# Attention block with FFN on one core: v ahead of q and k, the next norm in steps behind v's tiles, weight sums only in the attention

## The chip, the cores and the metric

The kernel runs on one core of a Trainium2 chip. The metric is the device time in microseconds of one execution; the time given is the median of several executions. The engines are named as in the profile: PE is TensorE (PEld its weight loads), DVE VectorE, ACT ScalarE, POOL GpSimd, SP SyncE. SP computes nothing here and issues DMAs on a hardware queue (q1 in the profile); DMAs issued from POOL go through a software queue (q0).

## The reference

x has the shape (2, 2048, 1024), that is 4096 tokens of H = 1024 in two batches. Everything is fp32.

```python
x = x + attn(layernorm(x), Wqkv, bqkv, Wo, bo)
x = x + ffn(layernorm(x), ...)

def attn(x, Wqkv, bqkv, Wo, bo):          # one head, D = 256
    qkv = x @ Wqkv + bqkv                 # (B, S, 3, 256)
    q, k, v = qkv[:, :, 0], qkv[:, :, 1], qkv[:, :, 2]
    p = softmax((q @ k.T) / sqrt(256))
    return (p @ v) @ Wo + bo

def ffn(h, ...):
    logits = h @ gate_w                   # 8 experts, the top 2 logits are summed
    w = sum(top_k(logits, 2))
    shared = (relu(h @ up_w) ** 2) @ down_w          # 1024 -> 2048 -> 1024
    routed = (((h @ fc1_w) @ expert_w) * w) @ fc2_w  # latent 512
    return layernorm(shared + routed) * ln_gamma + ln_beta
```

## The kernel before

**Matmuls in three passes.** TensorE gets every fp32 operand as a high part, rounded to its fp32r format, and a low part, the rest. `Pass3` (L117 to L138) adds high x high, high x low and low x high into one PSUM bank, so every product costs three matmuls; they are issued at L130. `split` (L140) makes the two parts: a cast on ACT (L142) and a subtraction on DVE or POOL (L143). `split_late` (L149, L150) does the same a step later, at the next `flush`.

**Blocks.** The 4096 tokens are 8 blocks of 512 (`NBLK` = 8, four per batch, `BPB` = 4), each of NB = 4 tiles of 128 rows. The stages are: the q/k/v stage for all blocks, the attention for all blocks, the FFN. The q/k/v stage takes the second batch first (`order`), since the k and v of the first batch can stay in SBUF (`keep`) for the attention that comes first; those of the second are written to `k_d` and `v_d` in DRAM and read back.

**The norm of a block.** x must be normalised by row, and TensorE needs it transposed, with features on the partitions. `norm_block` does this with four tiles of rows: the statistics of a tile come from ACT (`Moments`: two passes with a sum as they go, L259 and L271) or from DVE (`Stats`: bn_stats, L178 and L180) in turn; ACT normalises a tile in place (L283); DVE transposes it in 32x32 squares (`transpose_write`, L213), and POOL writes it to a DRAM scratch `xt_d` (L218); `fetch_tile` (L224) reads the tile back so that the squares come into their places. `split_tile` (L230) then splits a fetched tile into the high and low x (xha, xla) of the block that comes next.

**q, k and v of a block.** `qkv_block` does q as two chunks of 128 features by 512 tokens (24 matmuls 128x512 each, 8 contraction chunks in three passes; PSUM name pq), then k in the same way, then v as four tiles of 128 tokens by 256 features (24 matmuls 128x256 each, name pv). They share a PSUM pool, `psa`, of four banks. ACT evicts q and k (bias added), DVE the low half of k and all of v. q goes to `q_d` from POOL's queue. A callback `after` is called behind k and behind each v tile. `a_block` fills it: behind k come the loads of the rows of block i+2 (on SP's queue) and the split of tiles 0 and 1 of the next block, behind v tile 0 that of tile 2, behind v tile 1 that of tile 3. The norm of the block after that is called when the whole block is through:

```python
for i in range(NBLK - 1):
    if i:
        xts = norm_block(rows)
    xT = a_block(i, xts, xT)
```

This loop runs under `tc.manual_schedule()`: on each engine the instructions stay in the order in which they are written. Block 7's `a_block`, the attention and all behind it are ordered by the framework's scheduler from the program's order and priorities. In block 7 the callback behind k issues the scores of attention block 0 and its softmax's first quarter, ahead of the v tiles.

**Before the loop.** `begin` multiplies expert_w into fc2_w (`fold`), loads and splits the three parts of Wqkv (w0, w1 and w2 for q, k and v; subtractions on POOL, DVE and POOL), and makes the first block's x. The folded weights are written to `fc2e` from POOL's queue behind block 0.

**Weight sums.** The FFN uses sums of quarters of its weights, which are made in DRAM by DMAs alone, from POOL's queue: `sum_step` copies (2.5 MB per step) and adds (again 2.5 MB, an accumulating DMA). There are 14 steps, 8 of them with an add. Three steps are issued in the loop behind blocks i = 4, 5 and 6; the rest in the attention, two for each n from 2 on, behind the last `bo` DMA of the output projection before:

```python
if k in (2, 8) and n > 1 and steps:
    with tc.issue_after(last[0].ins):
        sum_step(steps.pop(0))
```

**The attention.** Its loop runs n from 1 to 8: scores of block n (name ps) beside values of block n-1 (name po), 16 key tiles of 128 each, with the softmax in quarters; `row_max` uses two small transposing matmuls (pmx, pmb) and `finish` the sums (psum, L604). `project` (L615 on) multiplies by Wo (name pw), adds the residual row `xres` (loaded on SP, with `bo` added by a POOL DMA) and writes x1 on SP (L634). In the last pass, n = 8, the four tiles of the FFN's first block are fetched on SP (name xt) and split on ACT and DVE (xh L149, xl L150), between the softmax quarters of the last attention block.

Of the kernel before, what the change touches and what calls it, by code (L numbers as in the profile page):

```python
# [12 lines left out]
ALU = mybir.AluOpType  # L13
# [4 lines left out]
P = 128  # L18
# [7 lines left out]
def kernel(  # L26
# [60 lines left out]
    def row(name):  # L87
        return rp.tile([P, C], FP, tag="r", name=name)
# [4 lines left out]
    def bank(pool, name):  # L93
        return pool.tile([P, W], FP, tag="b", name=name)
# [116 lines left out]
    def transpose_write(r, q=nc.gpsimd):  # L211
        b = row("xblk")
        nc.vector.transpose(  # L213
            b.rearrange("p (q k i) -> p q k i", q=P // SQ, i=SQ),
            r.rearrange("p (k i q) -> p q k i", k=NCC, i=SQ),
        )
        d = dram.tile([P, C], FP, tag="xt", name="xt_d", bufs=8)
        q.dma_start(out=d, in_=b)  # L218
        return d

    def fetch_tile(d, q=nc.gpsimd):

        xt = row("xt")
        q.dma_start(  # L224
            out=xt.rearrange("p (a f) -> p a f", a=P // SQ),
            in_=d.rearrange("(a i) (q f) -> (i q) a f", i=SQ, q=P // SQ),
        )
        return xt
# [65 lines left out]
        def second(self):  # L294
            pass

    def norm_block(rows):

        xts, ds = [], []
        ms = [Stats(r) if t % 2 else Moments(r, "n") for t, r in enumerate(rows[:2])]  # L300
        ms[0].second()
        for t in range(NB):
            ms[t].normalise()
            if t == 0:
                ms.append(Moments(rows[2], "n"))
                ms[2].second()
            ds.append(transpose_write(rows[t]))
            if t:
                xts.append(fetch_tile(ds[t - 1]))
            else:  # L310
                ms.append(Stats(rows[3]))
        return xts + [fetch_tile(ds[-1])]

    def transpose_tile(r, t, xT):

# [81 lines left out]
    def hl(t):  # L397

        return t.rearrange("p (s n) -> p s n", s=2)

    def qkv_block(n, wqkv, xT, after):

        keep = n < BPB
        units = {a: (unit if n == BPB - 1 else ex_unit)(f"{a}{n}") for a in "kv"}
        q = row("q")
        for i, a in enumerate("qk"):
            for dc in range(NDC):
                f = i * NDC + dc
                pm = bank(psa, "pq")
                acc = Pass3(pm, NCC)  # L410
                for c in range(NCC):
                    acc.add(piece(wqkv[i], c, D, ts(dc, P)), x_chunk(xT, c))
                bias = bqk_sb[:, f : f + 1]
                if a == "q":
                    nc.scalar.activation(q[:, ts(dc, W)], pm, AF.Identity, bias=bias)
                else:
                    h, l = (hl(units[a])[:, s, ts(dc, W)] for s in range(2))
                    nc.scalar.activation(h, pm, AF.Identity, bias=bias)
                    nc.vector.scalar_tensor_tensor(l, pm, bias, f32(h), ALU.add, ALU.subtract)
            if a == "q":  # L420
                nc.gpsimd.dma_start(out=q_d[n], in_=q)
            elif not keep:
                nc.gpsimd.dma_start(out=k_d[n], in_=f32(units[a]))
        if keep:
            kv[n] = [units["k"], units["v"]]
        after(-1)
        for t in range(NB):
            pm = bank(psa, "pv")
            if t % 2 == 0:
                v = half("v")  # L430
            acc = Pass3(pm[:, :D], NCC)
            for c in range(NCC):
                acc.add(x_chunk(xT, c, ts(t, P)), piece(wqkv[2], c, D, slice(0, D)))
            vt = v[:, ts(t % 2, D)]
            nc.vector.tensor_tensor(vt, pm[:, :D], bv_sb, ALU.add)
            flush()
            split_late(vt, *(hl(units["v"])[:, s, ts(t, D)] for s in range(2)))
            after(t)
        flush()
        if not keep:  # L440
            nc.gpsimd.dma_start(out=v_d[n], in_=f32(units["v"]))

    order = list(range(BPB, NBLK)) + list(range(BPB))
    def begin(wqkv, xT):

        ew, f2_0 = (unit(a, FP) for a in ("ew", "f2_0"))
        ev = ew.rearrange("p (c n) -> p c n", n=LAT)
        for i in range(NLC):
            nc.sync.dma_start(out=ev[:, :, ts(i, P)], in_=cols(expert_w, i, P))
        for i in range(NLC):  # L450
            nc.sync.dma_start(out=f2_0[:, ts(i, W)], in_=fc2_w[ts(i, P), 0:W])
        f2 = [f2_0]
        first = load_block(xf, order[0])
        f2.append(load("f2_1", cols(fc2_w, 1, W))[1])
        ws = [load(f"w{i}", cols(Wqkv, i, D)) for i in range(2)]
        rows = load_block(xf, order[1])
        ws.append(load("w2", cols(Wqkv, 2, D)))
        nc.gpsimd.dma_start(out=bqk_sb, in_=bqkv[0 : 2 * D].rearrange("(f p) -> p f", p=P))
        nc.gpsimd.dma_start(out=bv_sb, in_=bqkv[2 * D : 3 * D].partition_broadcast(P))

        eh, el = unit("eh"), unit("el")
        for mc in range(NLC):
            pt = bank(psc, "pt")
            for lc in range(NLC):
                nc.tensor.transpose(pt[:, ts(lc, P)], ew[:, ds(lc * LAT + mc * P, P)], ident)
            split(pt, eh[:, ts(mc, LAT)], el[:, ts(mc, LAT)])

        def split_f2(h, eng):
            f2h, f2l = unit(f"f2h{h}"), unit(f"f2l{h}")
            for mc in range(NLC):  # L470
                split(f2[h][:, ts(mc, W)], f2h[:, ts(mc, W)], f2l[:, ts(mc, W)], eng)
            return f2h, f2l

        def fold(f2hl, first=None):
            accs = [Pass3(bank(psa, "pf"), NLC) for _ in range(NLC)]
            for mc in range(NLC):
                if first:
                    first(mc)
                for lc in range(NLC):
                    accs[lc].add(  # L480
                        piece((eh, el), mc, LAT, ts(lc, P)), piece(f2hl, mc, W, slice(0, W))
                    )
            return accs

        def folded(h, accs):
            r = unit(f"fold{h}", FP)
            for lc in range(NLC):
                nc.scalar.copy(r[:, ts(lc, W)], accs[lc].ps)
            return r

        accs = fold(split_f2(0, nc.vector))
        stats = [row_stats(first[0])]
        for t in range(NB):
            if t + 1 < NB:
                stats.append(row_stats(first[t + 1]))
            normalise(first[t], stats[t])
            if t == 0:
                f2hl = split_f2(1, nc.gpsimd)
            elif t == 2:
                wqkv.append(split_unit(*ws[0], nc.gpsimd))  # L500
        r = [folded(0, accs)]
        r.append(folded(1, fold(f2hl, lambda t: transpose_tile(first[t], t, xT))))
        wqkv.append(split_unit(*ws[1]))
        wqkv.append(split_unit(*ws[2], nc.gpsimd))
        return norm_block(rows), r


    def split_q(n, r):
# [124 lines left out]
                )  # L633
            nc.sync.dma_start(out=x1[n][ts(t, P), :], in_=r)  # L634

    def a_block(i, xts, xT):
        nxt = []

        def after(t):

            if i + 1 < NBLK:
                if t < 0:
                    nxt.append(new_xT(f"a{i}"))
                    if i + 2 < NBLK:
                        rows[:] = load_block(xf, order[i + 2])
                for a in {-1: (0, 1), 0: (2,), 1: (3,)}.get(t, ()):
                    split_tile(xts[a], a, nxt[0])
            elif t < 0:
                start(0, load_row(q_d[0]))
                for k in range(NKC):  # L650
                    scores(0, k)
                start(1, load_row(q_d[1]))
                row_max(0)
                softmax(0, 0)

        qkv_block(order[i], wqkv, xT, after)
        return nxt[0] if nxt else None

    wqkv, xT = [], new_xT("a")
    with tc.manual_schedule():  # L660
        xts, fold = begin(wqkv, xT)
        steps = list(range(len(COPIES)))
        rows = []
        for i in range(NBLK - 1):
            if i:
                xts = norm_block(rows)
            xT = a_block(i, xts, xT)
            if i == 0:
                for h in range(C // W):
                    nc.gpsimd.dma_start(  # L670
                        out=cols(fc2e, h, W), in_=fold[h].rearrange("p (c n) -> p c n", n=W)
                    )
            if i >= NBLK // 2:
                sum_step(steps.pop(0))
    a_block(NBLK - 1, None, xT)

    wo_f = [load_row(Wo[ts(dc, P), :]) for dc in range(NDC)]

# [550 lines left out]
```

## Time and profile before

| | us |
|---|---|
| median of 3 runs | 2451.09 (2450.27 to 2451.32) |
| the profiled execution | 2448.58 |
| its span | 2446.8 |
| PE busy | 2360.8 (96%) |
| DVE busy | 1500.3 (61%) |
| ACT busy | 1133.7 (46%) |
| POOL busy | 338.5 (14%) |
| mean granted TensorE clock | 0.987 |

The span is that of one execution as the hardware profiler saw it; the 1.8 us between it and the execution's own time lie around it. Busy time counts computing instructions and not the waits. In the profile a line number is that of the kernel as it ran; "a <- b" in a wait reads "a waited for b". A program name such as xt or pq is that of a tile. In lists of stretches the columns are the stretch, its length, the busy time of the engines, the granted clock as a share of full clock, the busy share of the 16 DMA engines and the rate in GB/s.

### The profile page before, as it was taken

What the parts mean: (1) busy time and instruction counts of PE and PEld (TensorE: products, weight loads), DVE (VectorE), ACT (ScalarE), POOL (GpSimd) and SP (SyncE); (2) the same over time, 40 slices, a digit from 0 to 9 for tenths busy, and PEclk for the clock granted to TensorE, in tenths of its full rate; (3) what the DMA queues carried; (4) which work ended last, traced back from release to release, by engine and by line L of the source; (5) the groups of instructions that cost most, each with busy time, mean ns of one, the idle gap of its engine ahead of it and who ended that gap; (6) DMA issues with size and microseconds to landing.
All of it is one profiled execution on the core that took longest, in us unless ns stands there. A gap on an engine that the chain in (4) does not pass through costs nothing.

```text
span 2446.8 us, 29266 instructions
## 1 busy us (share of the span) xinstructions
PE 2360.8 (96%) x10704; PEld 1928.1 (79%) x10704; DVE 1500.3 (61%) x2168; ACT 1133.7 (46%) x1846; POOL 338.5 (14%) x427
## 2 busy tenths in 40 slices
PE   8899999999998999999999999999999999999997
PEld 7787888888886778777777877777888877787885
DVE  5555548888886466677845457663446673434646
ACT  5455435555544553666553364544135454214234
POOL 3211210111110010111320001221000021000003
PEclk9999999999999999999999999999999999999998
DMA  5866747999996566677887778986557787555565
GB/s 196 290 236 235 268 120 190 261 327 320 294 283 184 201 227 189 207 253 240 287 276 234 241 253 311 325 293 227 192 186 269 256 313 247 188 195 181 192 220 201
DMA packets 221342, 587.73 MB, mean 240 GB/s; under 512 B 18272, under 2 KB 80224, under 8 KB 219152
## 3 DMA queue, kind: packets, MB, share of 16 engines
q1 hardware_dynamic: 155616, 346.60, 42.3%
q0 software_dynamic: 65584, 239.27, 30.8%
q8 instruction: 85, 1.39, 0.2%
q14 instruction: 57, 0.47, 0.1%
HBM read 432.70 MB, written 210.76 MB: 263 GB/s over the span
## 4 chain that ended last, share of the span: by engine, by line
PE 72%; DVE 8%; DMA 7%; ACT 6%; issue 5%; POOL 1%; SPq 0%; POOLq 0%; ACTq 0%; DVEq 0%
PE pu L130 27%; PE pd L130 21%; PE ps L130 7%; PE po L130 7%; PE pw L130 4%; DMA xt<-xt_d 3%; DVE xblk L213 2%; DMA w<-wt 2%; DVE sp L996 1%; ACT xrow L283 1%; PE pg L829 1%; DMA xt_d<-xblk 1%; PE pf L130 1%; PE pq L130 1%; ACT junk L271 1%
## 5 line engine op out<-in xcount | busy, mean ns | idle before, releaser
L130 PE MATMUL pd<-w,sp 128*128 128x512 f32 x3336 | 775.3, 393 | 23.0 <-DVE sp L996 15.5
L130 PEld LDWEIGHTS pd<-w,sp 128*128 128x128 f32 x3336 | 626.1, 189 | 171.7 <-DVE sp L996 29.0
L130 PE MATMUL pu<-xh,w 128*128 128x512 f32 x2240 | 693.0, 390 | 2.0 <-ACT h L1026 1.0
L130 PEld LDWEIGHTS pu<-xh,w 128*128 128x128 f32 x2240 | 419.1, 188 | 93.2 <-DVE w L780 2.3
L130 PE MATMUL pu<-xl,w 128*128 128x512 f32 x1120 | 436.5, 390 | 3.7 <-DVE xl L150 3.7
L996 DVE TENSOR_TENSOR sp<-h,sp 128x512 fp32r<-128x512 f32 x238 | 178.0, 755 | 118.1 <-ACT sp L991 117.9
L130 PEld LDWEIGHTS pu<-xl,w 128*128 128x128 f32 x1120 | 210.2, 188 | 49.1 <-DVE xl L150 5.4
L991 ACT CAST sp<-h 128x512 fp32r<-128x512 f32 x238 | 144.9, 618 | 178.8 <-PE pd L130 127.3
L772 ACT CAST w<-w 128x512 fp32r<-128x512 f32 x210 | 128.7, 617 | 176.3 <-DMA w<-wt 163.2
L780 DVE TENSOR_TENSOR w<-w 128x512 fp32r<-128x512 f32 x210 | 147.0, 705 | 90.7 <-ACT w L772 85.8
L130 PE MATMUL po<-p,v 128*128 128x512 f32 x768 | 197.0, 395 | 1.3 <-ACT p L142 1.2
L130 PE MATMUL ps<-q,k 128*128 128x512 f32 x768 | 195.1, 392 | 0.0
L130 PEld LDWEIGHTS po<-p,v 128*128 128x128 f32 x768 | 144.3, 190 | 31.8 <-ACT p L142 1.6
L130 PEld LDWEIGHTS ps<-q,k 128*128 128x128 f32 x768 | 142.5, 188 | 32.1 <-DVE max L547 1.9
L783 POOL DMA_DIRECT2D w_p<-w x140 | 75.1, 536 | 562.9 <-DVE w L780 471.6
L150 DVE TENSOR_TENSOR xl<-xt,xh 128x512 fp32r<-128x512 f32 x104 | 77.5, 746 | 120.9 <-ACT xh L149 120.7
L213 DVE STREAM_TRANSPOSE xblk<-xrow 128x1024 f32<-128x1024 f32 x60 | 120.5, 2008 | 39.0 <-ACT xrow L283 39.0
L944 ACT ACTIVATE h<-h 128x1024 f32<-128x1024 f32 x48 | 50.7, 1055 | 200.6 <-DVE h L1043 153.2
L542 ACT COPY s<-ps 128x512 f32<-128x512 f32 x128 | 75.1, 587 | 147.1 <-PE ps L130 146.8
L908 POOL TENSOR_TENSOR res<-res,gb 128x1024 f32<-128x1024 f32 x32 | 80.1, 2506 | 408.0 <-DMA res<-x 407.6
L130 PE MATMUL pq<-xha,w_h 128*128 128x512 f32 x256 | 104.5, 408 | 20.9 <-ACT xha L142 20.9
L547 DVE TENSOR_TENSOR max<-ps,max 128x512 f32<-128x512 f32 x120 | 82.5, 688 | 49.1 <-ACT s L542 48.7
(181 smaller groups left out, 3122.3 us busy)
## 6 DMA issues: line engine op xcount, KB each, us to landing
w<-w_p SPq DMA_DIRECT2D x350, 512.0 KB, 3.4
w_p<-w POOLq DMA_DIRECT2D x140, 512.0 KB, 4.2
w<-wt SPq DMA_DIRECT2D x210, 256.0 KB, 3.4
xt_d<-xblk POOLq DMA_DIRECT2D x56, 512.0 KB, 4.3
xt<-xt_d POOLq DMA_DIRECT2D x56, 512.0 KB, 7.0
wt<-in_L_ffn_up_w_dram POOLq DMA_DIRECT2D x9, 2048.0 KB, 25.4
wt<-in_L_ffn_down_w_dram POOLq DMA_DIRECT2D x9, 2048.0 KB, 32.5
xrow<-in_L_attn_x_dram SPq DMA_DIRECT2D x32, 512.0 KB, 6.3
```

What stands on the lines that cost most here:

```text
L130: nc.tensor.matmul(self.ps, lhsT=a, rhs=b, start=self.i == 0, stop=self.i == self.n - 1, skip_group_check=self.on,)
L150: late_ops.append(lambda: nc.vector.tensor_tensor(lo, t, f32(hi), ALU.subtract))
L213: nc.vector.transpose(b.rearrange("p (q k i) -> p q k i", q=P // SQ, i=SQ), r.rearrange("p (k i q) -> p q k i", k=NCC, i=SQ),)
L542: nc.scalar.copy(s["s"][k // 4][:, ts(k % 4, W)], pm)
L547: nc.vector.tensor_tensor(s["max"], pm, s["max"], ALU.max)
L772: nc.scalar.copy(w[:, 0:W], f32(w)[:, W : 2 * W])
L780: nc.vector.tensor_tensor(w[:, W : 2 * W], v[:, W : 2 * W], v[:, 0:W], ALU.subtract)
L783: nc.gpsimd.dma_start(out=kept[key], in_=w.bitcast(FP))
L908: nc.gpsimd.tensor_tensor(self.res, self.res, beta_sb, ALU.add)
L944: nc.scalar.activation(o, v, AF.Relu)
L991: nc.scalar.copy(t[:, 0:W], v)
L996: add(t[:, W : 2 * W], v, f32(t)[:, 0:W], ALU.subtract)
```

## The change

1. `norm_block` becomes a class, `NormBlock`, that does the same in five steps: step 0 the statistics and tile 0, steps 1 to 3 the other tiles with the fetch of the tile before each, step 4 the last fetch.
2. `qkv_block` takes a list of parts. In all blocks but the last it is the four v tiles, then q and k. Behind v tile j comes step j of the norm of the *next* block; behind v tile 3 also step 4, and then the loads of the rows of block i+2, now on POOL's queue.
3. The next block's x tiles 0, 1 and 2 are split behind q's second and k's two chunks, and its tile 3 behind the first v tile of that next block (`x3`).
4. The last block takes v tiles 0 and 1, then q and k, then the scores of attention block 0, then v tiles 2 and 3.
5. The v weights (w2) are loaded and split first, then w0 and w1; the subtractions are on POOL, DVE and POOL.
6. k and v of blocks that don't stay are both written at the end of the block.
7. No weight sum is issued in the q/k/v loop; all 14 steps run in the attention's slots, n = 2 to 8.

```diff
--- before.py
+++ after.py
@@ -294,22 +294,27 @@
         def second(self):
             pass
 
-    def norm_block(rows):
-
-        xts, ds = [], []
-        ms = [Stats(r) if t % 2 else Moments(r, "n") for t, r in enumerate(rows[:2])]
-        ms[0].second()
-        for t in range(NB):
-            ms[t].normalise()
+    class NormBlock:
+
+
+        def __init__(self, rows):
+            self.rows, self.x, self.d, self.m = rows, [], [], []
+
+        def step(self, t):
+            rows, m = self.rows, self.m
             if t == 0:
-                ms.append(Moments(rows[2], "n"))
-                ms[2].second()
-            ds.append(transpose_write(rows[t]))
+                m += [Moments(rows[0], "n"), Stats(rows[1])]
+                m[0].second()
+            if t < NB:
+                m[t].normalise()
+                if t == 0:
+                    m.append(Moments(rows[2], "n"))
+                    m[2].second()
+                self.d.append(transpose_write(rows[t]))
+                if t == 0:
+                    m.append(Stats(rows[3]))
             if t:
-                xts.append(fetch_tile(ds[t - 1]))
-            else:
-                ms.append(Stats(rows[3]))
-        return xts + [fetch_tile(ds[-1])]
+                self.x.append(fetch_tile(self.d[t - 1]))
 
     def transpose_tile(r, t, xT):
 
@@ -398,47 +403,54 @@
 
         return t.rearrange("p (s n) -> p s n", s=2)
 
-    def qkv_block(n, wqkv, xT, after):
+    def qkv_block(n, wqkv, xT, parts, after):
+
+
 
         keep = n < BPB
         units = {a: (unit if n == BPB - 1 else ex_unit)(f"{a}{n}") for a in "kv"}
-        q = row("q")
-        for i, a in enumerate("qk"):
-            for dc in range(NDC):
-                f = i * NDC + dc
-                pm = bank(psa, "pq")
-                acc = Pass3(pm, NCC)
-                for c in range(NCC):
-                    acc.add(piece(wqkv[i], c, D, ts(dc, P)), x_chunk(xT, c))
-                bias = bqk_sb[:, f : f + 1]
-                if a == "q":
-                    nc.scalar.activation(q[:, ts(dc, W)], pm, AF.Identity, bias=bias)
-                else:
-                    h, l = (hl(units[a])[:, s, ts(dc, W)] for s in range(2))
-                    nc.scalar.activation(h, pm, AF.Identity, bias=bias)
-                    nc.vector.scalar_tensor_tensor(l, pm, bias, f32(h), ALU.add, ALU.subtract)
-            if a == "q":
-                nc.gpsimd.dma_start(out=q_d[n], in_=q)
-            elif not keep:
-                nc.gpsimd.dma_start(out=k_d[n], in_=f32(units[a]))
         if keep:
             kv[n] = [units["k"], units["v"]]
-        after(-1)
-        for t in range(NB):
+        got = {}
+
+        def v_tile(t):
             pm = bank(psa, "pv")
             if t % 2 == 0:
-                v = half("v")
+                got["v"] = half("v")
             acc = Pass3(pm[:, :D], NCC)
             for c in range(NCC):
                 acc.add(x_chunk(xT, c, ts(t, P)), piece(wqkv[2], c, D, slice(0, D)))
-            vt = v[:, ts(t % 2, D)]
+            vt = got["v"][:, ts(t % 2, D)]
             nc.vector.tensor_tensor(vt, pm[:, :D], bv_sb, ALU.add)
             flush()
             split_late(vt, *(hl(units["v"])[:, s, ts(t, D)] for s in range(2)))
-            after(t)
+
+        def qk_chunk(a, dc):
+            i = "qk".index(a)
+            pm = bank(psa, "pq")
+            acc = Pass3(pm, NCC)
+            for c in range(NCC):
+                acc.add(piece(wqkv[i], c, D, ts(dc, P)), x_chunk(xT, c))
+            bias = bqk_sb[:, i * NDC + dc : i * NDC + dc + 1]
+            flush()
+            if a == "q":
+                if dc == 0:
+                    got["q"] = row("q")
+                nc.scalar.activation(got["q"][:, ts(dc, W)], pm, AF.Identity, bias=bias)
+            else:
+                h, l = (hl(units[a])[:, s, ts(dc, W)] for s in range(2))
+                nc.scalar.activation(h, pm, AF.Identity, bias=bias)
+                nc.vector.scalar_tensor_tensor(l, pm, bias, f32(h), ALU.add, ALU.subtract)
+
+        for j, (a, i) in enumerate(parts):
+            v_tile(i) if a == "v" else qk_chunk(a, i)
+            if (a, i) == ("q", NDC - 1):
+                nc.gpsimd.dma_start(out=q_d[n], in_=got["q"])
+            after(j)
         flush()
         if not keep:
-            nc.gpsimd.dma_start(out=v_d[n], in_=f32(units["v"]))
+            for a, d in (("k", k_d), ("v", v_d)):
+                nc.gpsimd.dma_start(out=d[n], in_=f32(units[a]))
 
     order = list(range(BPB, NBLK)) + list(range(BPB))
     def begin(wqkv, xT):
@@ -452,9 +464,10 @@
         f2 = [f2_0]
         first = load_block(xf, order[0])
         f2.append(load("f2_1", cols(fc2_w, 1, W))[1])
-        ws = [load(f"w{i}", cols(Wqkv, i, D)) for i in range(2)]
+
+        ws = {i: load(f"w{i}", cols(Wqkv, i, D)) for i in (2, 0)}
         rows = load_block(xf, order[1])
-        ws.append(load("w2", cols(Wqkv, 2, D)))
+        ws[1] = load("w1", cols(Wqkv, 1, D))
         nc.gpsimd.dma_start(out=bqk_sb, in_=bqkv[0 : 2 * D].rearrange("(f p) -> p f", p=P))
         nc.gpsimd.dma_start(out=bv_sb, in_=bqkv[2 * D : 3 * D].partition_broadcast(P))
 
@@ -497,12 +510,12 @@
             if t == 0:
                 f2hl = split_f2(1, nc.gpsimd)
             elif t == 2:
-                wqkv.append(split_unit(*ws[0], nc.gpsimd))
+                wqkv[2] = split_unit(*ws[2], nc.gpsimd)
         r = [folded(0, accs)]
         r.append(folded(1, fold(f2hl, lambda t: transpose_tile(first[t], t, xT))))
-        wqkv.append(split_unit(*ws[1]))
-        wqkv.append(split_unit(*ws[2], nc.gpsimd))
-        return norm_block(rows), r
+        wqkv[0] = split_unit(*ws[0])
+        wqkv[1] = split_unit(*ws[1], nc.gpsimd)
+        return NormBlock(rows), r
 
 
     def split_q(n, r):
@@ -633,46 +646,57 @@
                 )
             nc.sync.dma_start(out=x1[n][ts(t, P), :], in_=r)
 
-    def a_block(i, xts, xT):
+    V = [("v", t) for t in range(NB)]
+    QK = [(a, dc) for a in "qk" for dc in range(NDC)]
+
+    def a_block(i, norm, xT, x3):
+
+
         nxt = []
-
-        def after(t):
-
-            if i + 1 < NBLK:
-                if t < 0:
-                    nxt.append(new_xT(f"a{i}"))
-                    if i + 2 < NBLK:
-                        rows[:] = load_block(xf, order[i + 2])
-                for a in {-1: (0, 1), 0: (2,), 1: (3,)}.get(t, ()):
-                    split_tile(xts[a], a, nxt[0])
-            elif t < 0:
-                start(0, load_row(q_d[0]))
-                for k in range(NKC):
-                    scores(0, k)
-                start(1, load_row(q_d[1]))
-                row_max(0)
-                softmax(0, 0)
-
-        qkv_block(order[i], wqkv, xT, after)
-        return nxt[0] if nxt else None
-
-    wqkv, xT = [], new_xT("a")
+        after_next = []
+
+        def after(j):
+            if i + 1 == NBLK:
+                if j == 0:
+                    x3()
+                elif j == NB + 1:
+                    start(0, load_row(q_d[0]))
+                    for k in range(NKC):
+                        scores(0, k)
+                    start(1, load_row(q_d[1]))
+                    row_max(0)
+                    softmax(0, 0)
+                return
+            if j == 0:
+                x3()
+            if j < NB:
+                norm.step(j)
+            if j == NB - 1:
+                norm.step(NB)
+                if i + 2 < NBLK:
+                    after_next.append(NormBlock(load_block(xf, order[i + 2], nc.gpsimd)))
+                nxt.append(new_xT(f"a{i}"))
+            elif j > NB:
+                split_tile(norm.x[j - NB - 1], j - NB - 1, nxt[0])
+
+        parts = V + QK if i + 1 < NBLK else V[:2] + QK + V[2:]
+        qkv_block(order[i], wqkv, xT, parts, after)
+        if nxt:
+            return (after_next or [None])[0], nxt[0], lambda: split_tile(norm.x[3], 3, nxt[0])
+
+    wqkv, xT = {}, new_xT("a")
     with tc.manual_schedule():
-        xts, fold = begin(wqkv, xT)
+        norm, fold = begin(wqkv, xT)
+        x3 = lambda: None
         steps = list(range(len(COPIES)))
-        rows = []
         for i in range(NBLK - 1):
-            if i:
-                xts = norm_block(rows)
-            xT = a_block(i, xts, xT)
+            norm, xT, x3 = a_block(i, norm, xT, x3)
             if i == 0:
                 for h in range(C // W):
                     nc.gpsimd.dma_start(
                         out=cols(fc2e, h, W), in_=fold[h].rearrange("p (c n) -> p c n", n=W)
                     )
-            if i >= NBLK // 2:
-                sum_step(steps.pop(0))
-    a_block(NBLK - 1, None, xT)
+    a_block(NBLK - 1, None, xT, x3)
 
     wo_f = [load_row(Wo[ts(dc, P), :]) for dc in range(NDC)]
```

## Prediction

> **What bounds the kernel now.** I read the page first, then TensorE's waits, the chain of waits through the q/k/v stage (38 to 329 us) and through the end of the attention (740 to 805 us), and last stretches of a few microseconds. The page:
>
> ```profile
> PE 2360.8 (96%) x10704; PEld 1928.1 (79%) x10704; DVE 1500.3 (61%) x2168; ACT 1133.7 (46%) x1846; POOL 338.5 (14%) x427
> DMA  5866747999996566677887778986557787555565
> ```
>
> TensorE is the bound nearly everywhere, so only its idle time and its slow clock can be won. In the DMA row a slice is 61 us: the q/k/v stage lies in slices 1 to 5, the attention in 6 to 13, and slices 12 and 13 (734 to 856 us) are the least loaded of the attention. TensorE's waits (total us, times, longest):
>
> ```profile
> PE pq L130 <- ACT xha L142: 20.9, 7, 6.0
> PE psum L604 <- DVE sum L580: 9.3, 1, 9.3
> ```
>
> The first is the stage that is changed: seven of eight blocks start by waiting for their split x. The gaps ahead of them, from one block's last pv to the next pq, are 5.99, 1.78, 1.74, 1.24, 4.70, 0.91 and 4.53 us, 20.9 in all. The second is at the end of the attention. The chain of waits before block 3 (start, us, what) says why the first wait exists:
>
> ```profile
> 137.94 2.03 DVE xblk L213
> 139.96 0.29 issue
> 140.25 6.95 DMA xt_d<-xblk
> 147.28 0.51 issue
> 147.78 6.22 DMA xt<-xt_d
> 154.03 0.63 ACT xha L142
> ```
>
> The norm starts at 120.70, after the last v tile of the block before has been evicted; 19.3 us of statistics and transposes, then 14 us of DMA through DRAM. TensorE restarts after such a gap at a lower clock (stretch, its us, TensorE busy, granted clock, DMA share, GB/s):
>
> ```profile
> 80.30:84.30 4.00, 3.96 (x9) 0.50 0.28 114
> 117.50:121.50 4.00, 3.97 (x10) 0.62 0.41 173
> 154.70:158.50 3.80, 3.80 (x10) 0.67 0.48 201
> 191.40:195.40 4.00, 4.00 (x16) 1.00 0.40 170
> ```
>
> Full clock is 16 matmuls in 4 us, half clock 9.
>
> **The change part by part.** The sum is made against the profiled run, 2448.58 us; the median, 2451.09, is 2.5 higher, and I add that at the end.
>
> *q/k/v loop.* One block's TensorE work is 96 matmuls 128x512 at 0.227 (21.8 us) and 96 of 128x256 at 0.12 (11.5), so 33.3 us. The block starts go from 38.96 to 304.94, a cadence of 38.0; the difference is 3.0 of gap and about 1.7 of slow clock and late pieces. With v first, a v tile needs only its own x tile, and the norm starts behind v0, some 22 us earlier in the block, under the matmuls of q and k. Then TensorE no longer sets the cadence alone; a loop does: rows landed, norm, writes, fetches, row loads behind the last fetch on POOL's queue, rows landed. I walk it: norm 19.3 us (120.70 to 139.96) plus the evictions of v tiles that now lie between its steps on DVE (about 4 x 0.8 = 3.2), 22.5; last xt_d write 0.3 issue and 4.0 (2.9 alone at 127.96, 6.95 in the chain); fetch 0.5 and 5.7 (4.9 alone, 6.2 to 8.7 with company); the rows land 1.3 behind the fetch (q's write, issued directly behind a fetch at 147.78, lands 1.3 after it). Together 34.2, ends 33 to 39. So cadence 34, first blocks 33.3. Starts by this walk: 38.96, 72.3, 105.6, 138.9, 172.9, 207.1, 241.3, 275.5. In the last block v0 and v1 run, then q0 waits for x tile 3 until 283.9 (2.6 us), and k1 ends at 306.8; before it ended at 329.18. Two v tiles more are done by then (5.8 us). Gain to there: 22.4 + 5.8 = 28.2.
>
> *Scores and softmax inside the last block.* Only v2 and v3 are left behind the scores and maxima: 5.8 us less cover for the softmax chain. Before, from the maxima (356.7) the low half of the first p came at 364.9 and the first po at 367.5, with pv to 364.9 between. Now pv ends about 2 us after its start plus 2.7 of the next scores, against 5.9 needed for the high half. About 3 us are lost: 25 stay.
>
> *Clock.* The part of this gain that is clock depends on when a gap counts. The rows above show 0.62 and 0.67 after gaps of 1.78 and 1.74, so five of seven gaps cost about 2 us each. [...] The trace decides, 25, and it also means that new gaps of 2 us in the loop would cost double.
>
> *Row loads on POOL's queue.* 24 loads leave SP's queue for POOL's: 4 x 0.53 us of issue a block on an engine with 14% busy, nothing. They now queue behind the fetch, and ahead of the writes of k and v (and, in the first block, of fc2e, 4.5 MB together) before the next block's first xt_d write. [...] The trace has 512 KB alone at 2.9 us from POOL (write at 127.96) and 2.9 from SP (x1 write at 759.39): I take nothing, and only the place in the queue costs.
>
> *w2 first, then w0, w1.* w0's low half is ready on DVE near 43.9 and q0 comes at 50.5; w1's on POOL near 48.4 and k0 comes at 61.4. The v and q matmuls hide it; without that cover it would be up to 5 us once. k_d and v_d together at the block's end, one flush more: nothing, blocks 4 to 7's k and v are read only in the attention.
>
> *Weight sums.* 55 MB of copy and add on POOL's queue stay 55, but 7.5 of them leave the q/k/v stage. By block n of the attention loop, before: 7.5, 10, 7.5, 10, 7.5, 5, 0 MB (n=2 to 8); after: 5, 5, 10, 7.5, 10, 10, 7.5. Leaving the q/k/v stage is part of the cadence above (transfers near their uncontended times). What counts is the end. Before, the last stretch has no sums (us, TensorE, load, DVE, ACT, POOL, clock, DMA share, GB/s):
>
> ```profile
> 748.00:756.00 8.00, 8.00 (x48) 6.67 (x47) 5.75 (x8) 3.77 (x6) 0.00 (x0) 1.00 0.01 2
> 764.00:772.00 8.00, 8.00 (x37) 6.61 (x36) 8.00 (x9) 2.68 (x3) 0.00 (x0) 1.00 0.97 312
> ```
>
> and the x1 writes and xt fetches (759.4 to 768.6, landing in 2.9 to 6.5 us) have the chip's DMA for themselves. The queues, first from 590 to 627 us, under sums, then from 759 to 776 us:
>
> ```profile
> q0 software_dynamic: 2274, 5.89, 66.0%
> q1 hardware_dynamic: 1584, 5.77, 40.4%
> ...
> q1 hardware_dynamic: 2984, 5.30, 91.0%
> ```
>
> With sums SP's queue gets 5.77 MB in 37 us, 156 GB/s; alone 312. Before, n=5's 10 MB took 56 us. After, n=7's 10 MB, issued from 684, end near 740; project(6)'s bo rows land near 750; then the 7.5 MB of n=8 run at 178 GB/s for 40 us, 753 to about 793, exactly over the x1 writes and xt fetches. Those 4 MB took 13 us at 312 and take 27 at 150: the last xt lands near 786 instead of 775. ACT has the copies of xt to xh (773.38, seven in a row) in order ahead of the exps of the last softmax, so it stands for 11 us; TensorE has 0.7 us of slack there and loses about 10, and 2 of slow clock behind it. The chain of this stretch before:
>
> ```profile
> 755.68 11.05 PE pw L130 x48
> 766.73 16.39 PE po L130 x72
> 783.14 10.27 DMA w<-wt
> 797.04 3.54 PE psum L604 x16
> ```
>
> The weight load w<-wt (10.3 us, behind the attention's last matmuls) is there in both, moved by as much; the sums have ended by then. n=6 and n=7 have 10 MB each, as n=5 had before without stalling TensorE, so I put nothing there (0 to 2). Tail: +11.5, from 4 (xt fetches finish 4 later because the sums share unevenly) to 18 (w<-wt still overlaps sums, 10 becomes 17).
>
> Sum: -25 + 11.5 = -13.5 on 2448.6, so 2435; at the median 2437.6, say 2438.
>
> **The rivals.**
> A, the tail is unhurt: the sums end before 760, or copies from weights run over faster than n=5's. For: in 590 to 627 the total is 315 GB/s and later in it 420, so the sums may run quicker. Against: their issue waits for bo, and bo itself landed at 730 to 742 already. Time: 2451 - 25 = 2426.
> B, slower: the loop through POOL's queue is long. Place: row loads of 2 MB behind the last fetch, then k, v and the next write behind them. Price: each microsecond above 34.2 costs 5 us over the looped blocks (25 - 5 x (L - 34.2)), and with the tail at 11.5 it turns into a loss from L = 36.9. For it: writes of 6.95 and fetches of 6.2 to 8.7 in the trace; with both at those sizes L is 38.5. Against: these were taken with row loads and other writes at the same time. Time at 38.5: gain 3.5, +8, 2459.
> C, the stage gains, but 12 to 15 us only (loop near 36.5, or a norm step's wait in DVE's order that holds the eviction of a v tile and so a PSUM bank for q1), and the tail takes it back: 2447 to 2454, no change.
>
> **How the numbers follow.** A difference under 0.2% (4.9 us) can't be told from no change here. Main case 0.46 (2430 to 2445, faster), A 0.16 (faster), C 0.14 (no change mostly), B 0.24 (slower). The range reaches from A's 2426 up into B: 2426 to 2458. Chances: faster 0.62, same 0.14, slower 0.24.
>
> **What would show it.** Right: block starts 33.5 to 34.5 apart, pq waits for xha under 5 us in all, clock 1.00 at the starts, k1 of the last block near 307, row loads landing 1 to 2 us behind the last fetch. At the end: q0 queue busy in 753 to 793, xt fetches of SP landing in 12 us or more, a new wait of po for p or of ACT for xt of about 10 us, DMA slices 12 and 13 at 8 or 9. Wrong: starts 36 or more apart with pv waiting for xha (B), or the sums finished before 760 and psum's wait still near 9.3 (A). A wait of pq for v's add on DVE in the middle of each block would break the walk at its second step.

## The result and the profile after

| | us |
|---|---|
| before, median of 4 runs beside it | 2450.68 |
| after, median of 4 runs | 2462.7 (2460.34 to 2465.05) |
| ratio | 1.0051, 95% interval 1.0039 to 1.0063 |
| the profiled execution after, its span | 2460.34, 2458.5 |

Slower by 12 us, where 13 faster were forecast; the time lies above the range. The page after:

```profile
PE 2351.9 (96%) x10704; PEld 1921.1 (78%) x10704; DVE 1493.4 (61%) x2168; ACT 1132.2 (46%) x1846; POOL 350.8 (14%) x451
PEclk9999999999997899999999999999999999999998
DMA  5876555699999676586887778886557787555565
```

TensorE's busy time fell by 9 us, and the time still grew: idle time was added. Slice 12 of the DMA row (counted from 0) went from 6 to 9 and slice 13 from 5 to 6, and there the clock row has 7 and 8. TensorE's waits after (us in total, times, longest):

```profile
PE po L130 <- ACT p L142: 31.9, 2, 31.5
PE psum L617 <- DVE sum L593: 10.0, 1, 10.0
PE pq L130 <- ACT xha L142: 6.4, 1, 6.4
```

The 20.9 us of pq in seven pieces became one of 6.4, ahead of the last block's q. A new wait of 31.5 us stands where there was none of this size. Counted from points that both traces have:

| point | before | after | after less before |
|---|---|---|---|
| first po of the attention | 367.5 | 344.9 | -22.6 |
| psum of attention block 6 | 753.8 | 731.7 | -22.1 |
| psum of attention block 7 | 797.0 | 809.5 | +12.5 |
| last matmul of the FFN (pd) | 2433.4 | 2444.7 | +11.3 |

The q/k/v stage gained 22 us and kept them through the attention; its last pass lost 34.6; the FFN changed by 1. Of the 34.6, 30.3 are the longer wait of po for p (31.5 against 1.2), 0.7 the longer wait of psum, and some 3, by estimate, the slow clock behind the gap (granted clock 0.50 from 790 to 796 us). The starts of the stage's blocks, clock and DMA (stretch, its us, TensorE busy, granted clock, DMA share, GB/s):

```profile
72.50:76.50 4.00, 4.00 (x35) 1.00 1.00 395
105.80:109.80 4.00, 4.00 (x33) 1.00 0.96 322
139.30:143.30 4.00, 3.66 (x29) 1.00 0.95 320
287.40:291.40 4.00, 3.98 (x9) 0.50 0.96 339
```

The first three are v tiles (shorter matmuls, hence more of them) at full clock; the last is q0 of block 7 behind its 6.4 us gap, at half clock. The chain of waits through the loss (start, us, what):

```profile
745.79 4.11 PE po L130 x17
749.89 36.32 DMA xt<-xt_d
...
786.76 1.65 ACT xh L142 x3
788.41 0.96 ACT s L585
789.37 0.51 ACT xh L142
789.88 0.96 ACT p L142
...
790.88 5.50 PE po L130 x12
```

The fourth xt fetch takes 36 us instead of 6.5. Behind it in ACT's order stand the copies to xh, and behind these the exp and the p that TensorE waits for. The two queues in 750 to 760 us (packets, which are the single entries of the DMA record, MB, share of the 16 DMA engines' time):

```profile
q0 software_dynamic: 654, 2.55, 71.4%
q1 hardware_dynamic: 655, 1.03, 28.6%
```

The queues moved nearly the same number of packets in this stretch, 654 and 655, but 2.55 MB against 1.03. The sums' packets are of 4 KB; the fetches' are of 1 KB.

### The profile page after: what moved, and what is told of

It reads as the page before. It is cut to its first block, busy times and chain, and to the rows that moved or that the text cites. A ratio compares the mean times of both kernels' runs of the same rounds, so it can differ in the third digit from the quotient of the medians.

```text
span 2458.5 us, 29234 instructions
## 1 busy us (share of the span) xinstructions
PE 2351.9 (96%) x10704; PEld 1921.1 (78%) x10704; DVE 1493.4 (61%) x2168; ACT 1132.2 (46%) x1846; POOL 350.8 (14%) x451
## 4 chain that ended last, share of the span: by engine, by line
PE 66%; DMA 11%; DVE 8%; issue 8%; ACT 6%; POOL 1%; another core or an unknown queue 0%; SPq 0%; POOLq 0%; ACTq 0%; DVEq 0%
PE pu L130 27%; PE pd L130 21%; PE ps L130 5%; PE po L130 5%; PE pw L130 3%; DMA w<-wt 2%; DMA xt<-xt_d 2%; DVE xblk L213 2%; DMA xres<-in_L_attn_bo_dram 2%; DVE sp L1020 1%; PE pg L853 1%; DMA wt<-in_L_ffn_down_w_dram 1%; PE pq L130 1%; PE pf L130 1%; ACT xrow L283 1%
## 5 line engine op out<-in xcount | busy, mean ns | idle before, releaser
L1020 DVE TENSOR_TENSOR sp<-h,sp 128x512 fp32r<-128x512 f32 x238 | 169.9, 721 | 119.6 <-ACT sp L1015 119.5
```

Of the source, the lines that this page charges most:

```text
L1020: add(t[:, W : 2 * W], v, f32(t)[:, 0:W], ALU.subtract)
```

## The experiments

**Is the tail the whole loss? Sums back in the loop (after_early).**

```diff
             norm, xT, x3 = a_block(i, norm, xT, x3)
...
+            if i >= NBLK // 2:
+                sum_step(steps.pop(0))
```

> The changed kernel with three sum steps put back behind the blocks i = 4, 5 and 6 of the q/k/v loop, as before. Theory: the tail stall of 31.5 us goes; in the loop each 2.5 MB step stands in POOL's queue ahead of the next block's first xt_d write, for 3 to 5 us of three block starts: 2428 + 8 to 15, that is 2436 to 2443. Rival (the loop is near its limit and takes each step's full 8 to 9 us, and the row loads too): 2450 to 2456.

Measured: 2429.04 us, ratio to before 0.9904 (0.9885 to 0.9922). The po wait is 1.5 us, the last xt fetch lands in 6.0. Psum of block 6 is at 732.2, against 731.7 in the changed kernel; so the three steps in the loop cost nothing that shows, less than the 8 to 15 expected, and the block starts stay 34 us apart. With 2429 against 2462.7, the place of the three steps decides whether the change gains or loses.

**The sums' part alone (before_late).**

```diff
-            if i >= NBLK // 2:
-                sum_step(steps.pop(0))
```

> The kernel before with one part of the change alone: no sum step in the q/k/v loop, all 14 in the attention. Theory: the tail loses what it loses in the changed kernel (+31 to +35 us), and the q/k/v loop gains 3 to 8 because the gaps of 4.70 and 4.53 us ahead of the blocks with sums shrink: 2451 + 34 - 5, that is 2474 to 2482. Rival (the tail only suffers together with the other parts, for instance since the attention starts 22 us earlier): 2443 to 2450.

Measured: 2489.22 us, 1.0152 (1.0129 to 1.0174), 38 us slower than before. Its waits:

```profile
PE po L130 <- ACT p L142: 29.8, 1, 29.8
PE pq L130 <- ACT xha L142: 19.5, 7, 5.0
```

The tail loses the same without the other parts: from psum of block 6 to that of block 7 it takes 78.9 us, against 43.2 before and 77.8 in the changed kernel. The loop got nothing for it: 19.5 us of pq waits against 20.9.

**Other slots for the sums (sums_by_n7).**

```diff
-            if k in (2, 8) and n > 1 and steps:
+            if (k in (2, 8) or k == 5 and n < 4) and n > 1 and steps:
```

> The changed kernel with a third slot (k = 5) in n = 2 and n = 3, so that all 14 sum steps are issued by n = 7 and none in the last pass. Theory (the sums of n = 8 share the DMA engines with the x1 writes and xt fetches of the last pass, and nothing else went wrong): the last xt fetches land in 4 to 8 us instead of 15 to 36, TensorE's wait of po for ACT p falls from 31.9 us to under 2, and the time falls by 31 to 35 us, to 2428 to 2432. Rival 1 (the stall belongs to the new order in the last pass or to the earlier start of the attention): the wait stays, 2458 to 2463. Rival 2 (55 MB do not fit into six passes; n = 3 with 12.5 MB delays bo and so x1): the wait moves to an earlier project, 2437 to 2450.

Measured: 2443.48 us, 0.9961 (0.9949 to 0.9973). The last fetches land in 4.3 to 7.1 us and the big po wait is gone, but rival 2 is right as well: `bo` rows issued from 650 to 669 us behind the sums take 30 to 41 us, pw waits 4.9 us for xres, and psum of blocks 5 and 6 comes at 679.9 and 744.9 instead of 674.3 and 731.7. With these slots the 55 MB do not fit ahead of the last pass without a loss.

**The sums behind the fetches (sums_behind).**

```diff
-            if k in (2, 8) and n > 1 and steps:
+            if k in (2, 8) and 1 < n < NBLK and steps:
...
         project(n - 1)
+    for i in steps:
+        with tc.issue_after(last[0].ins):
+            sum_step(i)
```

> The changed kernel with the sum steps 12 and 13 (7.5 MB, those of the last pass) issued only behind the last bo loads, after the xt fetches; nothing else is changed. They are down-projection sums and are first read some 200 us later. Theory (place, not bytes: what counts is that the sums run over the xt fetches): the fetches land in 4 to 7 us, no wait of po for p over 2 us; the sums now run over the first weight loads of the FFN, whose wait grows by 2 to 10 us: 2430 to 2440. Rival (7.5 MB cost the same wherever they run near the end): 2450 to 2465.

Measured: 2457.74 us, 1.0021 (1.0012 to 1.0031). The fetches are nearly free (6.2 to 8.4 us, 4 to 7 expected), but the loss moved. The step of its chain:

```profile
771.44 35.95 DMA w<-wt
```

and the queues from 780 to 800 us:

```profile
q0 software_dynamic: 1188, 4.65, 90.3%
q1 hardware_dynamic: 1188, 0.59, 12.3%
```

The load w<-wt, which took 10.3 us before, takes 36. It moves packets of 512 bytes, and for 1188 packets each the sums got 4.65 MB and the load 0.59. Behind it psum waits 20.2 us (10.2 in after_early), po another 4.6 and pw 3.7. The expected growth of 2 to 10 us was sized by bytes, and was wrong by the same error as the prediction; the time lies in the rival's range.

**Smaller packets in the sums (tail_1k).**

```diff
-            nc.gpsimd.dma_start(out=o, in_=t)
+            nc.gpsimd.dma_start(out=o, in_=t, max_dma_last_dim=1024 if i > 11 else 4096)
...
-                nc.gpsimd.dma_start(out=o, in_=t, accum_op=ALU.add, max_dma_last_dim=4096)
+                nc.gpsimd.dma_start(out=o, in_=t, accum_op=ALU.add, max_dma_last_dim=1024 if i > 11 else 4096)
```

> The changed kernel, the sum steps 12 and 13 (those of the last pass) cut into pieces of at most 1 KB instead of up to 4 KB; the same bytes. Theory (the two queues take turns packet by packet, and the xt fetches move 1 KB packets against the sums' 4 KB, so they get a fifth of the bytes): with equal packets SP's queue gets half or more, the last xt fetch lands in 16 to 24 us instead of 36, TensorE's wait falls from 31.5 to 10 to 19 us, 2440 to 2450. Rival (the share is one of bytes, or the xt fetches wait for x1 writes or for DRAM): the wait stays within 4 us of 31.5, 2458 to 2466.

Measured: 2465.07 us (ratio to before 1.0052, 1.0033 to 1.0072), no gain. The last fetch lands in 27.8 us instead of 36.3, the longest po wait is 22.9 instead of 31.5: the share moved, by less than expected. Until about 760 us the sums' packets are still of 4 KB; 2.6 MB of them come in 1 KB, and last, which is the size and the place of the add (2.5 MB): so the cut seems to have taken hold there and not in the copies. From 768 to 784 us nearly all are of 1 KB:

```profile
q0 software_dynamic: 1521, 1.59, 60.0%
q1 hardware_dynamic: 1522, 2.85, 54.2%
```

The counts are equal again, 1521 and 1522, and now SP's queue has more of the bytes, 2.85 MB against 1.59. But the sums then run at 100 GB/s, last longer, and meet the w<-wt load: the psum wait grew from 10.0 to 16.7. What the fetches got, the load gave back.

**Copies that nothing reads (extra_4k, extra_1k), on top of after_early.**

```diff
+            if n == NBLK and k == 2:
+                with tc.issue_after(last[0].ins):
+                    for e in range(5):
+                        nc.gpsimd.dma_start(
+                            out=dram.tile([W, C], FP, name=f"extra{e}"),
+                            in_=down_w[ts(e % 4, W), :], max_dma_last_dim=4096,
+                        )
```

In extra_1k the last number is 1024.

> The changed kernel with three sum steps in the q/k/v loop (2429 us, no sums in the last pass), and in the last pass five extra copies of 2 MB that nothing reads, from POOL's queue, in pieces of 4 KB. They stand in for sums and bring no dependence with them. Theory (what costs is the sharing of DMA time with the 1 KB packets of the xt fetches): the last fetch lands in 20 to 35 us instead of 6, TensorE waits 15 to 30 us for p, 2445 to 2462. Rival (the stall of the changed kernel came through the sums' own results or semaphores): within 5 us of 2429.

> The same five extra copies of 2 MB in pieces of 1 KB: order and bytes are the same, only the packets of POOL's queue are four times as many. Theory (the queues take turns by packet): the share of SP's queue during the fetches rises from about 90 GB/s to 130 to 160, the last fetch lands 8 to 15 us earlier than with 4 KB, and TensorE's wait for p is 8 to 15 us shorter. Rival (turns by bytes or by time): the fetches land within 3 us of those with 4 KB.

Measured: 2440.62 and 2443.76 us; the last fetch lands in 17.5 and 17.9 us, the longest po wait is 10.4 and 10.8. Bytes on the other queue are enough; no dependence on the sums is needed. The size is below what was expected: these copies ran at about 300 GB/s from 716 us on, so some 6 of their 10 MB had moved before the first fetch was issued at 737.9, and the last copy landed at 758 (extra_4k). The pair itself tells nothing of packets: in the trace of extra_1k the copies' packets are of 4 KB all the same (from 744 to 752 us 549 packets of POOL's queue for 2.18 MB).

**q and k first again (qk_first), on top of after_early.**

```diff
-        parts = V + QK if i + 1 < NBLK else V[:2] + QK + V[2:]
+        parts = QK + V
```

X tile 3 is split behind the last v tile, and in the last block all four v tiles come behind the scores.

> The changed kernel with three sum steps in the q/k/v loop (2429 us), and q and k ahead of v again in every block; the norm in steps, now behind q's and k's chunks, the row loads on POOL's queue and the w2-first loads stay. x tile 3 is split behind the last v tile. Theory (the gain of the stage is that a v tile needs one x tile while q needs all four, so that the last tiles' DMA and split lie behind v tiles): the block starts go back to 38 to 41 us apart, and 22 to 45 us are lost, 2450 to 2475. Rival (the gain is the norm in steps, wherever q and k stand): starts stay at 34 to 35.5 apart, 2429 to 2440.

Measured: 2469.61 us, 1.0072 (1.0052 to 1.0092), 41 us slower than after_early. Starts are 37.7 to 42.9 apart, against 38.0 before; pq waits 26.8 us for xha in seven pieces. The norm in steps and the row loads behind the last fetch give nothing while q0 needs all four x tiles.

**Row loads on SP again (rows_sp_early), on top of after_early.**

```diff
-    after_next.append(NormBlock(load_block(xf, order[i + 2], nc.gpsimd)))
+    after_next.append(NormBlock(load_block(xf, order[i + 2])))
```

> The changed kernel with three sum steps in the q/k/v loop (2429 us), and the row loads of the loop on SP's queue again, at the same place in the program (so that they start as soon as their buffers are free, not behind the last fetch). Theory of the prediction's walk (the loop through the row loads behind the fetch sets the cadence of 34.0): starts go to 33.3 to 33.6 apart from block 3 on, up to 3 us faster, 2426 to 2429. Rival 1 (the 0.7 us over 33.3 are late xla pieces of x tiles in v, not the rows): the same starts, 2428 to 2431. Rival 2 (the rows now collide with the xt_d writes and fetches, as they did before): starts 34.5 to 36 apart, 2432 to 2445.

Measured: 2457.53 us, 1.0021 (1.0014 to 1.0029), 28 us slower than after_early, beyond even rival 2. Starts are 38 to 39 apart. From its chain of waits:

```profile
146.27 7.09 DMA xt_d<-xblk
```

and from TensorE's waits:

```profile
PE pv L130 <- ACT xha L142: 17.3, 6, 3.3
```

On SP's queue the loads start when their buffers are free, at 141.79, in the middle of the writes and fetches. The last two xt_d writes of a block then land in about 7 us each instead of 2.9, and the fetches take 8 and 6 instead of 4.8. Behind the last fetch on POOL's queue they start late: in the changed kernel the first is issued at 138.64 and lands at 143.63, after that fetch (142.37). A run with SP's loads held back until the last fetch was not made, so that it is their time and not the kind of queue rests on these times in the traces. So v ahead of q and k alone, and the place of the row loads alone, each end near 38 us a block; only both together give 34.

**The last block's loads behind its last fetch (loads_pool), on top of after_early.** In the changed kernel the last block is the one in which SP still loads something during the fetches: q rows at 270.06 and Wo at 277.61. The chain there (changed kernel):

```profile
270.32 7.26 DMA xt_d<-xblk
...
277.63 0.51 issue
278.14 6.98 DMA xt<-xt_d
...
285.14 1.14 ACT xha L142 x2
```

```diff
-    start(0, load_row(q_d[0]))
+    start(0, load_row(q_d[0], nc.gpsimd))
...
-    start(1, load_row(q_d[1]))
+    start(1, load_row(q_d[1], nc.gpsimd))
...
-    wo_f = [load_row(Wo[ts(dc, P), :]) for dc in range(NDC)]
+    wo_f = [load_row(Wo[ts(dc, P), :], nc.gpsimd) for dc in range(NDC)]
```

> The changed kernel with three sum steps in the q/k/v loop (2429 us), and in the last block the loads of q_d for attention blocks 0 and 1 and of Wo on POOL's queue instead of SP's, so that they come behind the last fetch, as the row loads of the other blocks do. Theory (a load that starts on SP's queue while the last xt_d writes and fetches run makes each of them 4 us longer, as the row loads do): the last xt_d write lands in 3 us instead of 7.0, the last fetch in 5 instead of 7.1, q0's wait for x tile 3 falls from 6.1 to 2 to 3.5 us, 2425 to 2427. Rival 1 (the sum step on POOL's queue or the writes of q make these long): the same wait, 2428 to 2431. Rival 2 (the loads now stand behind the 2.5 MB of the sum step, and the scores wait for q): slower, 2432 to 2440.

Measured: 2420.64 us, 0.9866 (0.9848 to 0.9884), 8.4 us faster than after_early (in the traces the first po comes 7.9 us sooner after the last block's start): the last write lands in 2.9 us, the last fetch in 5.1, q0 waits 0.1, and its clock is full (1.00 from 281.4 to 285.4 us; its matmuls take 389 ns in the mean behind 285, where those of after_early take 416 to 425). This is the fastest version, 1.3% below before.

**One v tile more ahead of q (loads_pool_v3).**

```diff
-                elif j == NB + 1:
+                elif j == NB + 2:
...
-        parts = V + QK if i + 1 < NBLK else V[:2] + QK + V[2:]
+        parts = V + QK if i + 1 < NBLK else V[:3] + QK + V[3:]
```

> The kernel loads_pool with three v tiles ahead of q and k in the last block, and one behind the scores. Theory: v tile 2 (2.9 us) fills the rest of q0's wait for x tile 3, and the softmax behind the scores has 2.9 us less cover; the stall of q0 disappears (under 1 us) and its clock stays full (q and k in 21.6 us instead of 23.7), and up to 2 us come back at the first po: 0 to 4 us faster than loads_pool. Rival (the cover counts more, since po waits for p): 1 to 3 us slower than loads_pool, with a wait of po for p of 2 us or more.

Measured: 2428.96 us, 0.9900 (0.9884 to 0.9915), 8 us slower than loads_pool. With no wait left at q0 the tile fills nothing there, and its 2.9 us are missing behind the scores: po waits 4.0 us for p (0.4 in loads_pool), and the clock after it is slow (0.57 from 342 to 346 us; the po matmuls up to 350 take 446 ns in the mean, against 395 in loads_pool). The rival is right, by more than it said: some 5.4 us lie here in the two traces, and the rest was not followed.

## Why the prediction was wrong

**The walk of the loop was right.** Forecast starts of blocks 1 to 7: 72.3, 105.6, 138.9, 172.9, 207.1, 241.3, 275.5. Measured, the first v matmul: 72.5, 105.8, 139.3, 173.3, 207.2, 241.2, 275.2. The row loads' issues are 34.0 us apart in the mean, against L = 34.2, the loop's length in the prediction. The norm was some 1.7 longer than assumed (about 24 from the rows' landing to the last transpose), the last write and fetch shorter (2.9, and 4.3 to 5.5), so that the sum came out right by errors that cancel. Its reason was partly wrong: the norm does not start "some 22 us earlier in the block"; it starts 6.5 us after the block's start (78.99, with 72.5), and before it started after 3.2 (120.70, with 117.5). What is gained is that v asks for one x tile at a time, and that writes and fetches have the DMA to themselves. The clock was rightly taken from the trace: from 38 to 285 us the granted clock is 1.00 in the changed kernel, where TensorE's only listed wait is 1.4 us of pv in four pieces, and 0.96 before, with six of the seven pq gaps in that stretch.

**The row loads' place was taken as a price; it is half of the gain.** The prediction put that price at 0, from equal landings of 512 KB alone, 2.9 us from either queue. rows_sp_early says 28 us for POOL's queue. Landing times of one transfer alone could not show that: what counts here is which transfers it runs over. Its rival B took just the right numbers (6.95, fetches to 8.7, L = 38.5); they describe the loop with SP's loads, not the one with POOL's.

**The last block.** q0 was forecast at 283.9 and came at 287.4; k1's end at 306.8 became some 311.7: 3.5 us are the later q0, and the rest slow clock, since q and k took 24.2 us behind the gap, where the sum had 22.9 and the blocks before took 22.0. loads_pool shows the cause: SP's loads over the last write and fetch. The softmax's loss, put at 3 us, was about 0.7: from k1's end to the first po it took 33.2 us, against 38.3 less the 5.8 of two v tiles before. TensorE stands still for only 0.4 us ahead of the first po; why the softmax needs less cover than forecast was not followed. The two misses, 4.9 us late and 2.3 early, leave -22.6 instead of -25.

**The tail is the step that failed.** The mechanism, its place and its order (sums over x1 writes and xt fetches, ACT held, po waiting for p) were as forecast; the term was 34.6 us instead of 11.5, outside its own bounds of 4 to 18. The faulty line is "Those 4 MB took 13 us at 312 and take 27 at 150". They took 46.5 us (739.7 to 786.2), 90 GB/s. The 150 came from 590 to 627 us, where SP's queue moved 4 KB packets against 2 to 4 KB of the sums (1584 packets and 5.77 MB against 2274 and 5.89). In the four stretches below the counts of packets are equal within 1%, and the bytes are not:

| stretch | packets of q0 and q1 | MB of q0 and q1 | packet of q1 |
|---|---|---|---|
| changed kernel, 640 to 656 | 750, 751 | 2.92, 2.74 | 4 KB |
| changed kernel, 750 to 760 | 654, 655 | 2.55, 1.03 | 1 and 4 KB |
| sums_behind, 780 to 800 | 1188, 1188 | 4.65, 0.59 | 512 B |
| tail_1k, 768 to 784 | 1521, 1522 | 1.59, 2.85 | 1 and 4 KB, q0 1 KB |

That the queues take turns is the author's reading of these counts; how the turns are made was not shown, and 590 to 627 us has unequal counts. The prediction did not weigh such counts against the size of the packets, which the trace before has from 759 to 776 us:

```profile
DMA packets 2985, 5.32 MB, mean 313 GB/s; under 512 B 154, under 2 KB 2202, under 8 KB 2984
```

The 2048 packets between 512 B and 2 KB are the 2.1 MB of xt, in pieces of 1 KB. By estimate, equal counts of 1 KB and 4 KB packets leave the fetches a fifth of some 300 GB/s (313 in the view above), 60 GB/s, so 35 us; 2.1 MB of x1 writes at 150 are 14 more. That is 49 us, for what took 46.5. A second, smaller part: the sums ended at 784.7; the forecast 793 is 771 when the 22 us of gain are taken off. The counts are not equal to the end: in the changed kernel q0 and q1 moved 427 and 425 packets from 762 to 772 us, but 213 and 1182 from 774 to 784, while the last two adds on POOL's queue ran out (they land at 781.0 and 784.7). Whether the end of the adds is the reason is not shown.

**The rivals.** A (tail unhurt) is out. B had the right sign from the wrong place. Sums leaving the q/k/v stage were thought to be part of the gain; after_early and before_late show that they were worth nothing there.

## What to carry to other kernels

When two queues are busy, count packets and not only bytes: in the changed kernel from 750 to 760 us SP's queue, with the fetch in 1 KB packets beside the sums' 4 KB, had 655 packets against 654, and 1.03 MB against 2.55. So look at the packet size of each transfer on the critical path before background traffic is moved over it. Put background copies where the foreground has slack or packets as large; here that was the loop (after_early, 2429.04 us), not the end (2462.7). A queue's order is a tool as well: a load that is not urgent, put behind the last urgent transfer on the same queue, did not overtake it here (in the changed kernel the first row lands 1.2 to 1.6 us after the last fetch), and that was worth 28 us in the loop and 8 in the last block.

## What the hardware showed beyond what was expected

In the four stretches of the table two busy queues moved equal numbers of packets to within 1%, with packets from equal sizes (750 and 751 packets, 2.92 and 2.74 MB) down to 512 bytes against 4 KB (1188 and 1188, 0.59 and 4.65 MB), where a load of 10.3 us took 36. Cutting plain copies between DRAM tensors into 1 KB pieces left packets of 4 KB in the trace (extra_1k, 2.18 MB in 549 packets). With row loads on another queue at the same time (rows_sp_early) a 512 KB write landed in 7.1 us, where it took 2.9 without them (changed kernel).
